# Eight list tiles beside the first sort, the sort's prefix sums re-placed, and a third product added on VectorE

## The chip, the cores and the metric

The kernel runs on one core of a Trainium2 chip. The metric is the device time of one execution in microseconds (us). TensorE is called PE, VectorE DVE, ScalarE ACT, GpSimd POOL and SyncE SP. Times inside a run are counted from the start of the profiled span.

## The reference

One graph-attention layer over 4096 nodes with 512 features and 8 heads. The adjacency matrix `adj` (4096 x 4096, int32) is sparse: each row has some 10 to 40 non-zero entries, and only these take part in the row's softmax.

```python
hs = layer_norm(x, ln1);  ht = layer_norm(h_target, ln1)      # both masked by nodemask
q = (ht @ Wq + bq) / 8;  k = hs @ Wk + bk;  v = hs @ Wv + bv  # 8 heads of 64
probs = softmax(where(adj != 0, q @ k.T, -1e30))              # per head
ht = ht + (probs @ v) @ Wo + bo
ht = layer_norm(ht, ln2)
y = ht + gelu(ht @ W1) @ W2
out = layernorm(x + y)
```

## The kernel before

All matrix products are in fp32. Rows are taken in tiles of 128.

**Lists.** `edges(i)` reads the adjacency of row tile i in four quarters of 128 x 1024 int32 (512 KB each, issued on SP by `quarter`, L714). ACT turns a quarter into signs (L733, into one of three `signs` places) and adds up the degree. DVE multiplies the signs by column numbers (L740), takes the eight largest of each segment (three L742 a quarter), and at the end of the tile decodes them and picks the 24 largest (the tail, L749 to L766) into a record. `rest_d` receives the leftovers (L773, on SP). Quarters lie in eight places of a ring; those of the last tile that is read ahead of attention lie in two `wide` places. The first 16 tiles are part A, the other 16 part B (`NA` is 16).

**Sort.** `sort(part)` orders a part's rows by degree: a one-hot matrix `oh` (L834), its column totals by a matmul with ones (L845), a prefix scan on DVE (L846), a second matmul with a triangular matrix `lower` (L853), additions and a reduce, and a cast to the rank (L857). POOL then scatters the 16 records of 128 rows into DRAM (L861). After sorting, each tile of 128 rows has a known largest degree (its cap, 11 to 39), and tiles are taken in the order that `_order` gives: tiles 0 to 15 are of part A, 16 to 31 of part B. Two tiles make a feed-forward group.

**Projections.** `project` makes k and v of all 4096 rows: 16 steps of 2 tiles, with x loaded on SP (L882), normalised (DVE statistics, L697 to L692, POOL power L687, ACT L898), transposed and multiplied (L912, L937), copied by ACT (L939) and stored into `kvd` in DRAM.

**Attention.** For each tile, `front` fetches the rows of h_target that the records name, ties itself to the last projection (L1003, `latest`), normalises (ACT L1007), transposes (L1011, L1014) and multiplies with Wq (L1020, L1025). Then the edges are taken in groups of up to S = 3: POOL gathers one k and v row per node and edge from `kvd` (L975, 512 KB per gather, into 17 ring places for part A and 20 for part B), DVE multiplies with q (L1228) and reduces to logits (L1233), ACT takes the exponential (L1237, L1246), DVE multiplies the first two v rows by the probabilities (L1192), ACT the third (`by_scalar`, L1209 and L1212). In part B the first two products are added on DVE (L1196). PE adds the products up in PSUM by transposing matmuls (L1200), four of 128 x 128 per product that is left. `finish` and `feed` do the rest: Wo, norm, and the feed-forward with W1 and W2 (L1333, GELU on ACT L1336, L1342).

**Order.** `_weave` decides the order in which the parts are written: each part is a generator that yields a cost, and the one with the least cost so far goes on. First `projections`, `prepare` (part A's lists, sort, first fronts) and `fill` (the first `FILL` tiles of part B's lists) are woven; then attention, the feed-forward, `other_lists` (the other lists of part B, from cost `WAIT` = 100 on, then their sort) and late weights. A planner then orders each engine's queue; `behind(ins)` adds the constraint that an instruction comes after another one on its engine. Each queue runs in its order.

Of the kernel before, what the change touches and what calls it, by code (L numbers as in the profile page):

```python
# [8 lines left out]
F32 = mybir.dt.float32  # L9
# [3 lines left out]
ALU = mybir.AluOpType  # L13
# [4 lines left out]
P = 128  # L18
# [359 lines left out]
DEG, TGT, ROW, RST, E0 = 0, 1, 2, 3, 5  # L378
# [65 lines left out]
def adj_resnorm_kernel(  # L444
# [33 lines left out]
    nc = tc.nc  # L478
    N, D = x.shape
# [3 lines left out]
    NT = N // P  # L483
# [7 lines left out]
    SQ = 3  # L491
# [6 lines left out]
    for g in groups:  # L498
        i0 = GROUPS[-1][-1] + 1 if GROUPS else 0
        GROUPS.append(list(range(i0, i0 + len(g))))  # L500
    NA, NBT = len(CAPS_A), len(CAPS_B)
    PARTS = ((0, len(CAPS_A)), (len(CAPS_A), len(CAPS_B)))
    S = 3
# [29 lines left out]
    with tc.tile_pool(name="keep", bufs=1) as keep:  # L533
# [17 lines left out]
        with ExitStack() as late:  # L551
# [121 lines left out]
            def rstd_of(pool, mv, n, name):  # L673

                rs = power(pool, mv, n, name)
                return rs, negmean(pool, mv, rs, n, name)
# [6 lines left out]
            def power(pool, mv, n, name, ve=None):  # L683
                if ve is None:
                    ve = shifted(pool, mv, n, name)
                rs = pool.tile([P, n], F32, name=name + "_rs")
                nc.gpsimd.tensor_tensor(rs, ve, mhalf[:, :n], ALU.pow)  # L687
                return rs

            def negmean(pool, mv, rs, n, name):  # L690
                nm = pool.tile([P, n], F32, name=name + "_nm")
                nc.vector.scalar_tensor_tensor(nm, mv[:, :, 0], -1.0, rs, op0=ALU.mult, op1=ALU.mult)  # L692
                return nm
# [4 lines left out]
                nc.vector.bn_aggr(mv, st)  # L698


            held, moms = [], list(range(NT))
            mvh = wp.tile([P, NT, 2], F32, name="mvh")

            adjs = []
            DEEP = 8
            FILL = 6
            RINGED = NA + FILL - 1

            def quarter(i, h):
# [7 lines left out]
            def behind(ins):  # L717
                return tc.issue_after(ins[-1]) if ins else nullcontext()

            def edges(i):  # L720

                part = 1 if i >= NA else 0
                rec = Rs[part][:, i - PARTS[part][0], :]
                cand = lp.tile([P, SEG, 8], U16, name="cand", bufs=2)
                for h in range(NQ):
                    n = i * NQ + h
                    while len(adjs) < min(n + 2, NT * NQ):
                        adjs.append(quarter(*divmod(len(adjs), NQ)))
                    a, adjs[n] = adjs[n], None

                    sg = turn_of("signs", signs)
                    with behind(newest if i >= NA else []):
                        nc.scalar.activation(sg, a, AF.Sign, accum_out=dpart[:, i, h:h + 1])  # L733
                    ahead = min(n + DEEP - 1, n + 3 + n // 2)
                    while len(adjs) < min(max(n + 3, min(ahead, RINGED * NQ)), NT * NQ):
                        adjs.append(quarter(*divmod(len(adjs), NQ)))
                    yield 0.0 if i < NA else 1.0
                    wd = sg.bitcast(U16)
                    with behind(logits):
                        nc.vector.tensor_tensor(wd, wd, lio, ALU.mult)  # L740
                    for s, (w0, w1) in enumerate(SEGS):
                        nc.vector.max(cand[:, h * SQ + s, :], wd[:, w0:w1])  # L742
                    if h == 1:
                        keep_rest()
                    if h % 2 and moms:
                        moments(moms.pop(0))
                    yield 2.0 if i < NA else 1.0
                dec = dec_w
                nc.vector.tensor_single_scalar(dec[:, 0], cand, 255, op=ALU.bitwise_and)  # L749
                nc.vector.tensor_single_scalar(dec[:, 1], cand, 8, op=ALU.logical_shift_right)  # L750
                gid = lp.tile([P, 2 * SEG, 8], F32, name="gid")
                dec = dec.rearrange("p b s e -> p (b s) e")
                off = segoff.rearrange("p b q s -> p (b q s)")
                nc.vector.scalar_tensor_tensor(gid, dec, 0.0,
                                               off.unsqueeze(2).to_broadcast([P, 2 * SEG, 8]),
                                               op0=ALU.is_gt, op1=ALU.mult)
                nc.vector.scalar_tensor_tensor(gid, dec, 2.0, gid, op0=ALU.mult, op1=ALU.add)
                flat = gid.rearrange("p s e -> p (s e)")
                for r in range(RE // 8):
                    top = rec[:, E0 + r * 8:E0 + (r + 1) * 8]  # L760
                    nc.vector.max(top, flat)
                    if r + 1 < RE // 8:
                        nc.vector.match_replace(flat, top, flat, 0.0)
                held.append((rest_d[i * P:(i + 1) * P, :], flat))
                has = lp.tile([P, MAXE], F32, name="ehas")
                nc.vector.tensor_scalar(has[:, :RE], rec[:, E0:E0 + RE], 0.0, 0.0, op0=ALU.is_gt,  # L766
                                        op1=ALU.add, accum_out=cnt[:, i:i + 1])
                yield 4.0

            def keep_rest():  # L770

# [42 lines left out]
            def sort(part):  # L814
# [23 lines left out]
                pos = pos[:, :NB * n].rearrange("p (b i) -> p b i", b=NB)  # L838
                posf = pos.rearrange("p b i -> p (b i)")
                w = NB * n // 2  # L840
                yield 6.0
                for c in range(2):
                    sl = slice(c * w, (c + 1) * w)
                    pt = ps.tile([P, w], F32, name="t", bufs=2)
                    nc.tensor.matmul(pt, ones_bf, ohf[:, sl], start=True, stop=True)  # L845
                    nc.vector.tensor_tensor_scan(posf[:, sl], one_c.to_broadcast([P, w]), pt,  # L846
                                                 0.0 if c == 0 else posf[:, c * w - 1:c * w],
                                                 op0=ALU.mult, op1=ALU.add)
                yield 4.0
                for c in range(2):  # L850
                    sl = slice(c * w, (c + 1) * w)
# [323 lines left out]
            def attention():  # L1175
# [10 lines left out]
                def values(i, j0, n, kv, p, cps, after):  # L1186

                    m = n - 1 if n == S else n  # L1190
                    v4 = kv[:, :m, D:].rearrange("p j (h d) -> p j h d", h=H)
                    nc.vector.tensor_tensor(v4, v4, p[:, j0:j0 + m, :].unsqueeze(3)  # L1192
                                            .to_broadcast([P, m, H, HD]), ALU.mult)
                    slots = list(range(n))
                    if m > 1 and i >= NA:
                        nc.vector.tensor_add(kv[:, 0, D:], kv[:, 0, D:], kv[:, 1, D:])  # L1196
                        slots.remove(1)
                    for j in slots:
                        for c in range(KC):
                            nc.tensor.matmul(cps[:, c, :], kv[:, j, D + c * P:D + (c + 1) * P], ident,  # L1200
                                             is_transpose=True, start=j0 + j == 0 and c == 0,
                                             stop=j0 + n == TILES[i][1] and j == slots[-1],
                                             skip_group_check=True)
                    if after is not None:
                        tails.append(after)
# [181 lines left out]

            WAIT = 100.0
            AHEAD = 4
            UNIT = 60.0  # L1390

            ed = all_edges()
# [16 lines left out]
            def prepare():  # L1409

                yield from _take(ed, NA * steps)
                ready.append("lists")
                while moms:
                    moments(moms.pop(0))
                rs, nm = rstd_of(wp, mvh, NT, "n0")
                for R, (i0, n) in zip(Rs, PARTS):
                    Rf = R.bitcast(F32)
                    nc.vector.tensor_copy(Rf[:, :, RST], rs[:, i0:i0 + n])
                    nc.vector.tensor_copy(Rf[:, :, RST + 1], nm[:, i0:i0 + n])
                nm = turn_of("wide", wide)  # L1420
                nc.sync.dma_start(nm[:NT, :P], nodemask.rearrange("(c p) -> c p", p=P))
                nmf = nm.bitcast(F32)[:NT, P:2 * P]
                nc.vector.tensor_scalar(nmf, nm[:NT, :P], 1.0, None, op0=ALU.not_equal)
                nc.vector.tensor_reduce(bad[:NT, 0:1], nmf, AX.X, ALU.max)
                yield from sort(0)
                yield from first_fronts()

            def fill():

                while not ready:  # L1430
                    yield None
                yield 9.0
                for cost in _take(ed, FILL * steps):
                    yield cost

# [15 lines left out]

            def other_lists():
                for cost in ed:
                    yield 1.8 * cost
                keep_rest()
                yield from sort(1)

# [37 lines left out]
```

## Time and profile before

| | |
|---|---|
| three runs, median | 1816.04 us (1813.79 to 1820.43) |
| profiled execution | 1813.07 us, its span 1811.3 us |
| busy us: PE / DVE / ACT / POOL | 1678.3 / 1397.6 / 1224.7 / 967.4 |
| DMA | 461.03 MB, mean 255 GB/s |
| L1200, transposes into PSUM | x2008 |
| L1196, additions of two products | x101, 680 ns |
| last projection matmul ends | 267.5 us |
| first gather issued, first L1228 | 271.5 us, 295.3 us |

A busy share is an average over stages: projections and part A's lists up to about 267 us, then attention with the feed-forward beside it up to about 1670, then the feed-forward alone. Matmuls are pipelined, so a mean duration on PE is a latency and not the distance between two matmuls. Idle time on an engine that is not the bound costs nothing.

### The profile page before, as it was taken

To read this page: it belongs to the slowest core of one execution; us is meant where nothing else is said; L and a number is where in the kernel's file an instruction comes from. 1 tells how busy PE (TensorE), PEld (TensorE's weight loads), DVE (VectorE), ACT (ScalarE), POOL (GpSimd) and SP (SyncE) were. 2 spreads that over 40 slices of the span, in tenths; PEclk is the share of its full clock that TensorE was granted. 3 is DMA by queue.
4 is the path that set the end of the run, shared out by engine and by line. 5 is a ranking of instruction groups with operands and counts; after the bars stand their busy time and mean duration, and the time that the engine had idled before them with its cause. 6 is when DMAs were issued, how large, how long until landed. Compare 5 with 4: busy or idle time off the path is not lost. (4 is left out here: it accounts for less than half of the span.)

```text
span 1811.3 us, 22772 instructions
## 1 busy us (share of the span) xinstructions
PE 1678.3 (93%) x7030; PEld 1096.2 (61%) x7030; DVE 1397.6 (77%) x2404; ACT 1224.7 (68%) x3121; POOL 967.4 (53%) x818
## 2 busy tenths in 40 slices
PE   7999994697998999998999989989999999999995
PEld 3444442565665666675676756656666666666663
DVE  6887568989987879886969989897969797988100
ACT  5776464677786887675868767777858676776210
POOL 1000155756455556787677788867566665762101
PEclk9999995898999999999999999999999999999998
DMA  9999879888778697678788888777677776772000
GB/s 344 365 377 359 306 260 357 304 274 311 268 247 304 239 336 237 219 239 278 276 284 286 276 274 277 251 271 271 205 254 227 266 262 232 256 245 92 24 1 26
DMA packets 142060, 461.03 MB, mean 255 GB/s; under 512 B 18548, under 2 KB 23496, under 8 KB 141928
## 3 DMA queue, kind: packets, MB, share of 16 engines
q0 software_dynamic: 96144, 342.27, 55.6%
q1 hardware_dynamic: 37968, 94.12, 14.7%
q10 hardware_dynamic: 7816, 23.08, 3.3%
q8 instruction: 58, 0.95, 0.2%
q14 instruction: 74, 0.61, 0.1%
HBM read 430.61 MB, written 28.79 MB: 254 GB/s over the span
## 5 line engine op out<-in xcount | busy, mean ns | idle before, releaser
L975 POOL DMA_INDIRECT kv<-kvd,rec x603 | 753.4, 1249 | 355.8 <-PE cps L1200 166.5
L1333 PE MATMUL pf<-h2T,w 128*128 128x256 f32 (+1 forms) x2176 | 466.4, 368 | 0.6 <-ACT h2T L1155 0.6
L1342 PE MATMUL po<-w,gt 128*128 128x512 f32 x1024 | 461.4, 593 | 5.6 <-ACT gt L1336 5.6
L1333 PEld LDWEIGHTS pf<-h2T,w 128*128 128x128 f32 x2176 | 389.6, 191 | 64.9 <-issue 20.1
L1228 DVE TENSOR_TENSOR kv<-kv,tq 128x1536 f32<-128x1536 f32 (+2 forms) x211 | 351.6, 1676 | 61.9 <-DMA kv<-kvd,rec 49.2
L1212 ACT ACTIVATE kv<-kv,pa 128x64 f32<-128x64 f32 x1520 | 391.8, 337 | 4.6
L1233 DVE TENSOR_REDUCE lg<-kv 128x24 f32<-128x1536 f32 (+2 forms) x211 | 350.1, 1666 | 1.3
L1200 PE MATMUL cps<-ident,kv 128*128 128x128 f32 x2008 | 264.9, 280 | 47.0 <-DVE kv L1192 39.5
L1200 PEld LDWEIGHTS cps<-ident,kv 128*128 128x128 f32 x2008 | 239.1, 144 | 113.2 <-issue 44.6
L1342 PEld LDWEIGHTS po<-w,gt 128*128 128x128 f32 x1024 | 187.0, 190 | 198.9 <-issue 191.3
L1192 DVE TENSOR_TENSOR kv<-kv,p 128x1024 f32<-128x1024 f32 (+1 forms) x211 | 250.9, 1193 | 25.3 <-ACT p L1237 25.2
L687 POOL TENSOR_TENSOR n_rs<-n_ve,mhalf 128x2 f32<-128x2 f32 (+2 forms) x51 | 45.8, 897 | 337.2 <-DVE n_ve L680 172.8
L733 ACT ACTIVATE kv<-kv 128x1024 uint8<-128x1024 int32 x128 | 134.5, 1053 | 67.1 <-DMA kv<-in_adj_dram 34.6
L1020 PE MATMUL t<-wq,tq 128*128 128x512 f32 x256 | 126.1, 640 | 19.8 <-ACT tq L1014 19.8
L1336 ACT ACTIVATE gt<-pf 128x512 f32<-128x512 f32 x128 | 76.4, 597 | 93.8 <-PE pf L1333 90.3
L1336 ACT ACT_TABLE_LOAD x104 | 133.4, 1283 | 1.7
L937 PE MATMUL pq<-wk,h2T 128*128 128x512 f32 x256 | 118.7, 607 | 8.2 <-ACT tq L939 4.5
L937 PE MATMUL pq<-wv,h2T 128*128 128x512 f32 x256 | 115.4, 593 | 1.5 <-ACT tq L939 0.7
L1124 PE MATMUL t<-wo,rb 128*128 128x512 f32 x256 | 115.2, 593 | 0.0
L742 DVE MAX8 cand<-kv 128x8 uint16<-128x171 uint16 (+1 forms) x384 | 109.1, 324 | 1.2
L1237 ACT ACTIVATE p<-lg 128x24 f32<-128x24 f32 (+2 forms) x179 | 39.0, 218 | 100.1 <-DVE lg L1233 99.3
L1020 PEld LDWEIGHTS t<-wq,tq 128*128 128x128 f32 x256 | 51.3, 206 | 79.9 <-issue 47.0
(160 smaller groups left out, 1541.0 us busy)
## 6 DMA issues: line engine op xcount, KB each, us to landing
kv<-in_adj_dram SPq DMA_DIRECT2D x128, 512.0 KB, 7.1
kvd<-tq ACTq DMA_DIRECT2D x24, 512.0 KB, 6.9
kv<-kvd,rec POOLq DMA_INDIRECT x603, 5.9
kv<-in_L_gnn_h_target_dram SPq DMA_DIRECT2D x32, 256.0 KB, 7.2
kv<-in_x_dram SPq DMA_DIRECT2D x15, 512.0 KB, 8.7
w<-in_L_gnn_W_dram SPq DMA_DIRECT2D x4, 1024.0 KB, 12.4
kvd<-kv ACTq DMA_DIRECT2D x8, 512.0 KB, 3.2
w<-in_L_gnn_W_dram ACTq DMA_DIRECT2D x4, 1024.0 KB, 7.3
```

The lines of the kernel that those rows point to most:

```text
L733: nc.scalar.activation(sg, a, AF.Sign, accum_out=dpart[:, i, h:h + 1])
L937: nc.tensor.matmul(pkv, hT[:, kc, j * P:(j + 1) * P], w[:, kc, :], start=kc == 0, stop=kc == KC - 1)
L975: issues[:] = [nc.gpsimd.indirect_dma_start(out=dst, out_offset=None, in_=table[:, :], in_offset=bass.IndirectOffsetOnAxis(ap=idx, axis=0) ...
L1020: nc.tensor.matmul(pq, hT[:, kc, :], wq[:, kc, :], start=kc == 0, stop=kc == KC - 1)
L1192: nc.vector.tensor_tensor(v4, v4, p[:, j0:j0 + m, :].unsqueeze(3) .to_broadcast([P, m, H, HD]), ALU.mult)
L1200: nc.tensor.matmul(cps[:, c, :], kv[:, j, D + c * P:D + (c + 1) * P], ident, is_transpose=True, start=j0 + j == 0 and c == 0, stop=j0 + n ...
L1212: newest[:] = [nc.scalar.mul(v, v, pa[:, hd:hd + 1]).ins]
L1228: nc.vector.tensor_tensor(kv[:, :n, :D], kv[:, :n, :D], tq[:, :D].unsqueeze(1).to_broadcast([P, n, D]), ALU.mult)
L1233: logits[:] = [nc.vector.tensor_reduce(lg[:, :n, :], kv[:, :n, :D].rearrange("p j (h d) -> p j h d", h=H), AX.X, ALU.add).ins]
L1333: nc.tensor.matmul(pf[:, k, :], w1[(f0 + k) // KC][:, kc, (f0 + k) % KC * P:((f0 + k) % KC + 1) * P], h2T[:, kc, :w], start=kc == 0, stop= ...
L1336: nc.scalar.activation(gt, pf, AF.Gelu_apprx_tanh)
L1342: nc.tensor.matmul(po[j], gt[:, k, j * P:(j + 1) * P], w2[(f0 + k) // KC][:, (f0 + k) % KC, :], start=False, stop=f0 + k == FC - 1, skip_g ...
```

## The change

- `FILL` goes from 6 to 8: eight tiles of part B have their lists made ahead of attention. Their costs in the weave go down (quarters 0.7 and 0.7 instead of 1.0 and 1.0, the tail 2.4 instead of 4.0), `fill` starts at 1.0 instead of 9.0, and part A's quarters count 1.8 instead of 2.0. `other_lists` counts 2.2 instead of 1.8 times the cost.
- In the first sort both totals (L845) are written right after 2.0 instead of 6.0, into the PSUM places `cps`, and the scans come after another 6.0, behind the latest max (L742) of the lists.
- The layer-norm factors of h_target (L692 on 32 columns, L1418, L1419) are taken out of `prepare` and written behind the first sort's scans.
- From tile 21 on (`DENSE`), in every second full group of three, a further L1196 adds the third product to the sum on DVE, and PE transposes one product instead of two.

```diff
-            FILL = 6
+            FILL = 8
...
-                    yield 0.0 if i < NA else 1.0
+                    yield 0.0 if i < NA else 0.7 if i < NA + FILL else 1.0
...
-                        nc.vector.max(cand[:, h * SQ + s, :], wd[:, w0:w1])
+                        maxima[:] = [nc.vector.max(cand[:, h * SQ + s, :], wd[:, w0:w1]).ins]
...
-                    yield 2.0 if i < NA else 1.0
+                    yield 1.8 if i < NA else 0.7 if i < NA + FILL else 1.0
...
-                yield 4.0
+                yield 2.4 if NA <= i < NA + FILL else 4.0
...
-                yield 6.0
+                yield 6.0 if part else 2.0
+                tots = []
                 for c in range(2):
                     sl = slice(c * w, (c + 1) * w)
-                    pt = ps.tile([P, w], F32, name="t", bufs=2)
+                    pt = ps.tile([P, w], F32, name="t" if part else "cps", bufs=2)
                     nc.tensor.matmul(pt, ones_bf, ohf[:, sl], start=True, stop=True)
-                    nc.vector.tensor_tensor_scan(posf[:, sl], one_c.to_broadcast([P, w]), pt,
-                                                 0.0 if c == 0 else posf[:, c * w - 1:c * w],
-                                                 op0=ALU.mult, op1=ALU.add)
+                    tots.append((sl, pt))
+                if not part:
+                    yield 6.0
+                for c, (sl, pt) in enumerate(tots):
+                    with behind([] if part else maxima):
+                        scan = nc.vector.tensor_tensor_scan(
+                            posf[:, sl], one_c.to_broadcast([P, w]), pt,
+                            0.0 if c == 0 else posf[:, c * w - 1:c * w],
+                            op0=ALU.mult, op1=ALU.add)
+                while factors:
+                    with behind([scan.ins]):
+                        factors.pop()()
...
+                        if n == S and i >= DENSE and j0 // S % 2:
+                            nc.vector.tensor_add(kv[:, 0, D:], kv[:, 0, D:], kv[:, S - 1, D:])
+                            slots.remove(S - 1)
...
+            DENSE = 21
...
-                rs, nm = rstd_of(wp, mvh, NT, "n0")
-                for R, (i0, n) in zip(Rs, PARTS):
-                    Rf = R.bitcast(F32)
-                    nc.vector.tensor_copy(Rf[:, :, RST], rs[:, i0:i0 + n])
-                    nc.vector.tensor_copy(Rf[:, :, RST + 1], nm[:, i0:i0 + n])
+                rs = power(wp, mvh, NT, "n0")
+
+                def rest_of_factors():
+                    nm = negmean(wp, mvh, rs, NT, "n0")
+                    for R, (i0, n) in zip(Rs, PARTS):
+                        Rf = R.bitcast(F32)
+                        nc.vector.tensor_copy(Rf[:, :, RST], rs[:, i0:i0 + n])
+                        nc.vector.tensor_copy(Rf[:, :, RST + 1], nm[:, i0:i0 + n])
+
+                factors.append(rest_of_factors)
...
-                yield 9.0
+                yield 1.0
...
-                    yield 1.8 * cost
+                    yield 2.2 * cost
```

More of the change, by code (lines that the diff above doesn't have):

```diff
@@ L698, in stats @@
                 nc.vector.bn_aggr(mv, st)
-            held, moms = [], list(range(NT))
+            held, moms, factors, maxima = [], list(range(NT)), [], []
             mvh = wp.tile([P, NT, 2], F32, name="mvh")
```

## The prediction

> **What bounds the kernel now.** I read the page's 40 slices first, then the stages (busy time by window), then the timeline of each engine around the hole.
>
> ```profile
> PE   7999994697998999998999989989999999999995
> ...
> PEclk9999995898999999999999999999999999999998
> ```
>
> Each digit is a tenth of a 45.3 us slice. TensorE is nearly full except in slices 7 and 8, where its clock drops too. The stages say how much is lost, and how full the others are (columns: stage; its length, then PE, weight load, DVE, ACT and POOL busy us with instruction counts; clock; DMA share; GB/s):
>
> ```profile
> 200.00:250.00 50.00, 49.49 (x142) 23.54 (x141) 23.04 (x74) 24.58 (x47) 16.15 (x18) 1.00 0.70 250
> ...
> 270.00:290.00 20.00, 10.52 (x22) 4.30 (x20) 13.62 (x54) 12.75 (x28) 15.08 (x16) 0.72 0.92 334
> 290.00:310.00 20.00, 2.82 (x12) 2.42 (x12) 18.02 (x37) 7.14 (x25) 4.63 (x5) 0.50 0.99 376
> 310.00:330.00 20.00, 9.92 (x40) 7.91 (x41) 19.12 (x23) 8.37 (x32) 14.11 (x11) 0.59 0.97 368
> ...
> 1450.00:1550.00 100.00, 100.00 (x436) 68.56 (x435) 81.27 (x96) 73.51 (x201) 60.98 (x54) 1.00 0.74 247
> ```
>
> Between 270 and 330 PE stands idle for 60 - 23.3 = 36.7 us while DVE and DMA are full; between 200 and 250 DVE is half empty and DMA has 30% free. From 1350 to 1640 PE is full (289.8 of 290 us) and DVE is not. After attention (about 1670) PE runs only the feed-forward to the end. So PE is the bound, and its idle time before that moves the end. (The page's own chain covers the last 3 us only.) The hole in lines of the timelines (start, length, engine, line; in brackets the idle before and who ended it):
>
> ```profile
> 224.11 0.95 DVE L846 TENSOR_TENSOR_SCAN kv<-one_c,t 128x384 f32<-128x384 f32 x1 [13.01 <-PE t L845]
> 229.82 0.17 DVE L857 CAST kv<-kv 128x16 int32<-128x16 f32 x1
> 271.53 0.94 POOL L975 DMA_INDIRECT kv<-kvd,rec  x1 [0.56 <-issue]
> 289.83 1.06 ACT L733 ACTIVATE kv<-kv 128x1024 uint8<-128x1024 int32 x1 [5.50 <-DMA kv<-in_adj_dram]
> 295.34 1.74 DVE L1228 TENSOR_TENSOR kv<-kv,tq 128x1536 f32<-128x1536 f32 x1
> 305.25 2.82 PE L1200 MATMUL cps<-ident,kv 128*128 128x128 f32 x12 [21.88 <-DVE kv L1192]
> ```
>
> DVE waits 13.01 us for the sort's first matmul, which stands behind projections on PE. Projections end at 267.5 and the first gather leaves at 271.5, yet attention's first product (L1228) runs at 295.34: six lists of part B (235 to 294, 9.8 us each) lie ahead of it on DVE, and the last one's quarter reached ACT late. The sort itself is not the last wait: its records fetch h_target rows by 262.7, before the projections end.
>
> **What the Trainium skill says.** "TensorE: Matmul & The Clock Gate", What's actually happening: an idle window of about 3.4 us halves PE's clock; the trace agrees (0.50 in 290:310). The same page, Architectural detail: ACT and DVE are strict FIFO; here ACT's 5.50 us wait held all behind it. "VectorE: DVE Perf Modes", TRN2 errata: an fp32 tensor_tensor of 512 takes (512+151)/0.96 = 691 ns; L1196 has a median of 680. "DMA: Bandwidth & Descriptors", Issuing engines are not separate DMA queues: SP, ACT and POOL share 16 engines; here 400 to 419 GB/s from 285 to 305 with all three loading.
>
> **The change, part by part.** Line numbers are those of before; the walks use the changed program's engine order.
>
> (a) Eight lists instead of six ahead of attention, beginning where DVE idled. A list is 4 loads of 512 KB, 4 Signs (1053 + 191 ns), 4 scale-and-max rounds (1.17 us) and a tail (L749 to L766, 3.4 us; 252.09 to 255.47): 8.1 us of DVE alone. Mixed with another list's rounds it is less: 277.57 to 281.95 held a tail and two rounds, 4.4 us instead of 5.8. The new order mixes about half, so 7.2 us each.
> Signs of list 16 now follow the copies ready at 209.2, one batch behind each projection tile: about 211 instead of 233.8. DVE: four rounds to 217; sort arithmetic (two scans, two adds, product, reduce, cast, factors) 6.2 us within list 17; the cast at about 227 (before 229.82). Then seven lists, less the last one's two rounds and tail. That reaches `front`'s tie L1003 at 217 + 6.2 + 6.5 x 7.2 = 270, against 268.17.
> On ACT the last list's third and fourth Signs stand ahead of L1007. Their loads take places that its first two Signs free at 265; landing takes 7.2 us (as at 282.59 to 289.83), so both end at 274.7, and L1007 starts there, not at 268.62: 6 us late. From there, as before: transposes, L1014 2.87 us, L1020 for one tile 4.9 us; L1025 at 284.7 and L1228 at **285.4 instead of 295.3: 10 us earlier**. List 21's rest inside attention (296.99 to 312: 3.3 us and a wait of 0.91) is gone too: 14.
> But gathers set a second limit. They issue from about 273.5, one per 1.25 us; a gather is 0.5 MB, 1.25 us at 400 GB/s, and the 4 MB of late weights (ACT queue, after the first scalar products) take 10 us of it. The 17th lands at about 310. The seventh group, at 318.62 before, then runs at 308 to 312. I take **-9**, bounds -14 and -2.
>
> (b) Two lists less inside attention: 2 x 8 us of DVE and 2 x 5 us of ACT leave the stretch 375 to 850. There PE was idle 17 us (400:600) and 10.5 us (600:900), mostly for gathers and logits. Pace 2.2 on 8 lists (8 x 26.4 = 211 cost units) ends with 1.8 on 10 (216), so the second sort and its POOL scatters stay where they were. **-4**; bounds 0 and -8.
>
> (c) Three products added. Full groups of 3 with odd index in tiles 21 to 31: 28. Each drops 4 PE transposes and adds one DVE add.
>
> ```profile
> L1200 PE MATMUL cps<-ident,kv 128*128 128x128 f32 x2008 | 264.9, 280 | 47.0 <-DVE kv L1192 39.5 <-DVE kv L1196 7.3
> L1196 DVE TENSOR_TENSOR kv<-kv 128x512 f32<-128x512 f32 x101 | 68.4, 680 | 0.3
> ```
>
> 280 ns is a pipelined latency; eight transposes at 1454.11 hand over at 1454.98, so 0.109 us each: 112 x 0.109 = 12.2 us of PE. DVE pays 28 x 0.61 (its start-to-start) = 17 us. These tiles run from about 1177 to 1670. From 1350 on PE is full and DVE has 14 to 19% free, so two thirds count in full; from 1177 to 1350 DVE is 75 to 95% busy and the gain is doubtful. POOL already waits 34.4 us on L1196 (26 times) to reuse ring places; the added instruction lengthens that by 0.6 us per group, behind four groups of prefetch. **-10**; bounds -13 and +5 (all on DVE, less the PE time).
>
> (d) The sort. Its two totals move from 223.75 to about 209.2 on PE; `oh` was ready at 210.6. DVE no longer waits for the 5.43 us power ahead of it (L692 moves behind the scans), and the store that L754 waited for (to 205.78) stands ahead of the weight load on SP now, so `oh` comes at 204 to 210.6: PE stalls 0 to 1.5 us. New wait: the scans stand behind list 16's last max, and both L853 products need the PSUM places the scans free. PE reaches them at 217.7, the scans end at 218 and 219. Behind L853 on PE are the projections, and all of attention behind those. **+1**; bounds 0 and +6. The factors only have to be written before the scatters (L861). The last x load moves 4 adjacency loads back on SP, 2 MB or 5.5 us; its transposes (216) have 11 us of slack: 0, covered by PE's queued projections; without that cover up to 3 us inside (d)'s bound.
>
> Sum: -9 - 4 - 10 + 1 = **-22 us**. The profiled execution took 1813.07 us (span 1811.3 and 1.8 around it), so it becomes 1791. It lies 3.0 below the median of the runs, 1816.04; on the median's scale I predict **1794**.
>
> **Rivals.**
> Larger gain: gathers don't hold the ramp (-14), the lighter DVE fills PE's gaps (-8), all transposes count (-12), +1: -33, **1783**. For it: DVE waited only 0.88 us for gathers up to 330. Against: DMA already ran at 0.92 to 0.99 there.
> No change: the ramp is bound by transfers (-2), DVE takes back what lists free (-1), and the added products fall in groups where DVE comes last (-2): -5, **1811**. For it: DVE 92% busy in 1000:1200. Against: PE full from 1350.
> Slower: the lists pile up ahead of attention. DVE works them off in order ahead of the tie, and the three `signs` places hold ACT, with the projections' copies behind it, at DVE's pace. At today's 9.8 us a list the tie is at 217 + 6.2 + 6.5 x 9.8 = 287, and L1228, 15 us after the tie as in (a), at 302: 7 late. At 13 us it is at 323, 28 late; with -13 from the other parts that is +15, **1831**. It decides above some 12.1 us a list (L1228 22 late). For it: today's 9.8, and 4 MB more traffic before 270. Against: much of the 9.8 is waiting for ACT, whose Signs come earlier.
> That the change does nothing is excluded: the order shows eight lists and 112 fewer transposes.
>
> **How the numbers follow.** 0.5% is 9 us, about what a measurement of this kernel can tell from no change. Main case (1786 to 1805) 0.61, larger gain 0.14, no change 0.17, slower 0.08. So faster 0.75, same 0.17, slower 0.08. The range, 1777 to 1812, leaves out the slower case, the top of no change and the far end of the larger gain.
>
> **What would show it.** Right: L846 ends its 13.01 us wait at about 217; L857 near 227; first L1228 near 285; less than 30 us of PE idle in 270:330; 1896 transposes in L1200's group and PE still full from 1350. Wrong: the tie after 275, an ACT wait above 8 us on adjacency ahead of L1007, PE waiting at L853 by more than 3 us, or DVE above 95% with PE gaps after 1350.

## The result, and the profile after

The changed kernel takes 1803.15 us (median of 6 runs, 1799.61 to 1806.98), the kernel before beside it 1816.58 us (6 runs): ratio **0.9924**, interval 0.9905 to 0.9943, 13 us less. In a second comparison, beside three relatives, it took 1815.39 us against 1819.57 us: ratio **0.9979**, interval 0.9961 to 0.9997, 4 us less. The two intervals do not meet. So an interval covers the scatter of one comparison and not the difference between comparisons (whether the chip makes it is not shown). The kernel is faster by 4 to 13 us, and below, kernels are compared first with those measured beside them on the same chip. The profiled execution of after took 1805.56 us (span 1803.8).

Of the page of after, the same two rows of 40 slices (a slice is now 45.1 us). The hole in slices 7 and 8 is still there.

```profile
PE   7989984697999999998999999989999999999995
...
PEclk9999997898999999999999999989999999999998
```

The same stages by window (length, then busy us and counts of PE, weight load, DVE, ACT and POOL; clock; DMA share; GB/s):

```profile
200.00:250.00 50.00, 47.49 (x138) 22.46 (x137) 33.97 (x127) 30.16 (x58) 17.30 (x18) 1.00 0.93 330
270.00:290.00 20.00, 11.65 (x27) 5.31 (x26) 14.42 (x59) 11.95 (x24) 7.74 (x8) 0.74 0.76 254
290.00:310.00 20.00, 9.55 (x41) 6.41 (x40) 17.21 (x13) 7.34 (x31) 16.00 (x14) 0.89 1.03 406
310.00:330.00 20.00, 6.83 (x34) 6.03 (x32) 14.90 (x16) 7.71 (x30) 13.36 (x11) 0.51 1.03 401
1450.00:1550.00 100.00, 100.00 (x418) 67.05 (x417) 88.67 (x109) 74.88 (x202) 64.41 (x53) 1.00 0.75 250
```

DVE is no longer half empty in 200:250 (33.97 us instead of 23.04): the lists moved there. But PE now loses 2.5 us in that window and is idle for 32.0 us in 270:330 (36.7 before). From 290 to 330 the DMA engines are full at 401 to 406 GB/s and DVE is not. From 290 to 450 DVE waits 12.4 us for gathers, where before waited 6.7: more of the ramp waits for transfers.

Lines of after's timelines that answer to those of the hole before (start, length, engine, line; in brackets the idle before and who ended it):

```profile
216.41 0.93 DVE L852 TENSOR_TENSOR_SCAN kv<-one_c,cps 128x384 f32<-128x384 f32 x1
226.12 0.16 DVE L867 CAST kv<-kv 128x16 int32<-128x16 f32 x1
271.81 3.70 PE L947 MATMUL pq<-wv,h2T 128*128 128x512 f32 x8 [0.60 <-ACT kv L949]
282.58 0.94 POOL L985 DMA_INDIRECT kv<-kvd,rec  x1 [1.11 <-DMA kv<-in_adj_dram]
292.07 1.76 DVE L1241 TENSOR_TENSOR kv<-kv,tq 128x1536 f32<-128x1536 f32 x1 [0.71 <-DMA kv<-kvd,rec]
299.07 2.82 PE L1213 MATMUL cps<-ident,kv 128*128 128x128 f32 x12 [5.08 <-DVE kv L1202]
```

The 13.01 us that DVE waited for the totals are gone and the cast (L857, now L867) comes 3.7 us earlier. Yet the last projection ends at 271.81 + 3.70 = 275.5 instead of 267.5, the first gather leaves at 282.58 instead of 271.53, and the first product (L1228, now L1241) runs at 292.07 instead of 295.34, just after the gather that it needs.

The groups of the transposes and of the additions (L1200 and L1196, now L1213, L1206 and the new L1209; count, busy us, mean ns, idle before and its releasers):

```profile
L1213 PE MATMUL cps<-ident,kv 128*128 128x128 f32 x1896 | 252.5, 280 | 34.4 <-DVE kv L1202 23.6 <-DVE kv L1206 7.8 <-issue 2.5
L1206 DVE TENSOR_TENSOR kv<-kv 128x512 f32<-128x512 f32 x101 | 68.7, 684 | 0.3
L1209 DVE TENSOR_TENSOR kv<-kv 128x512 f32<-128x512 f32 x28 | 19.2, 685 | 0.1
```

112 transposes fewer and 28 additions more, as written.

### The profile page after: what moved, and what is told of

Same layout as the page of the kernel before. It is cut to its first block, busy times and chain, and to the rows that moved or that the text cites. A ratio compares the mean times of both kernels' runs of the same rounds, so it can differ in the third digit from the quotient of the medians.

```text
span 1803.8 us, 22591 instructions
## 1 busy us (share of the span) xinstructions
PE 1666.8 (92%) x6918; PEld 1081.8 (60%) x6918; DVE 1413.1 (78%) x2432; ACT 1224.5 (68%) x3121; POOL 971.4 (54%) x818
## 5 line engine op out<-in xcount | busy, mean ns | idle before, releaser
L1241 DVE TENSOR_TENSOR kv<-kv,tq 128x1536 f32<-128x1536 f32 (+2 forms) x211 | 352.0, 1677 | 78.7 <-DMA kv<-kvd,rec 63.1
L1213 PEld LDWEIGHTS cps<-ident,kv 128*128 128x128 f32 x1896 | 226.9, 145 | 99.5 <-issue 45.7
L1213 PE MATMUL cps<-ident,kv 128*128 128x128 f32 x1896 | 252.5, 280 | 34.4 <-DVE kv L1202 23.6
L687 POOL TENSOR_TENSOR n_rs<-n_ve,mhalf 128x2 f32<-128x2 f32 (+2 forms) x51 | 48.9, 958 | 345.1 <-DVE n_ve L680 153.6
L733 ACT ACTIVATE kv<-kv 128x1024 uint8<-128x1024 int32 x128 | 134.5, 1053 | 59.6 <-DMA kv<-in_adj_dram 22.3
L1134 PE MATMUL t<-wo,rb 128*128 128x512 f32 x256 | 115.5, 592 | 0.0
L742 DVE MAX8 cand<-kv 128x8 uint16<-128x171 uint16 (+1 forms) x384 | 108.2, 325 | 6.2 <-remote 2.4
```

What stands on the lines that cost most here:

```text
L1241: nc.vector.tensor_tensor(kv[:, :n, :D], kv[:, :n, :D], tq[:, :D].unsqueeze(1).to_broadcast([P, n, D]), ALU.mult)
```

## The experiments

Three groups of four kernels; each group ran on one chip, beside runs of the kernel before (medians 1818.87, 1819.57 and 1817.31 us). Gains in us below are (1 - ratio) times that median.

### First group: the parts one by one

**c_only**, the kernel before with part (c):

```diff
                         slots.remove(1)
+                        if n == S and i >= DENSE and j0 // S % 2:
+                            nc.vector.tensor_add(kv[:, 0, D:], kv[:, 0, D:], kv[:, S - 1, D:])
+                            slots.remove(S - 1)
```

> The kernel before with the third product's addition alone (DENSE = 21), lists and sort as before. Theory 1 (the whole gain is the 112 transposes, since between the two traces PE's busy time fell by 11.5 us and its idle time grew by 4): 10 to 13 us less than before, ratio 0.9930 to 0.9945, and the milestones of tiles 0 to 20 unmoved. Theory 2 (the products pay only because two lists fewer inside attention left DVE room): 0 to 5 us less, ratio 0.997 to 1.000, with new waits of PE for DVE after 1177 us.

Measured: 1813.1 us, ratio 0.9970 (0.9953 to 0.9988), 5.5 us less. Between the two theories; the added products pay without fewer lists, but about half of what they were forecast.

**no_c**, the changed kernel without them:

```diff
-                        if n == S and i >= DENSE and j0 // S % 2:
-                            nc.vector.tensor_add(kv[:, 0, D:], kv[:, 0, D:], kv[:, S - 1, D:])
-                            slots.remove(S - 1)
```

> The changed kernel without the third product's addition: eight lists and the re-placed sort remain. Theory 1: no gain or a small loss, 0 to 5 us more than before, ratio 1.000 to 1.003, last projection matmul still late, near 275 us. Theory 2 (lists and sort pay what the forecast said, -9 - 4 + 1): 12 us less, ratio 0.9935.

Measured: 1807.21 us, ratio 0.9938 (0.9913 to 0.9963), 11 us less. Theory 1 falls. It came from comparing PE's busy time in two single profiles, and that total is no steady quantity: after and after_again below have the same instructions and show 1666.8 and 1675.6 us.

**sort_only**, no_c with six lists and their old costs, so that the sort's change is left:

```diff
-            FILL = 8
+            FILL = 6
...
-                    yield 0.0 if i < NA else 0.7 if i < NA + FILL else 1.0
+                    yield 0.0 if i < NA else 1.0
...
-                    yield 1.8 if i < NA else 0.7 if i < NA + FILL else 1.0
+                    yield 2.0 if i < NA else 1.0
...
-                yield 2.4 if NA <= i < NA + FILL else 4.0
+                yield 4.0
...
-                yield 1.0
+                yield 9.0
...
-                    yield 2.2 * cost
+                    yield 1.8 * cost
```

> The kernel before with the sort's change alone (totals written after 2.0, factors behind the scans), six lists with their old costs. Theory 1: within 3 us of before, cast of the rank a few us earlier, projections ending at 267 to 269 us as before. Rival: the sort is what pays and the lists lose it again; then 5 us or more less than before, with the first gather earlier than 271.5 us.

Measured: 1818.63 us, ratio 0.9984 (0.9968 to 1.0001), within 3 us. The cast came at 233.7, not earlier than before.

**lists_only**, the opposite: the kernel before with these six lines as the change has them, and the old sort (two of the six are shown, the others are those of sort_only the other way round):

```diff
-            FILL = 6
+            FILL = 8
...
-                    yield 2.0 if i < NA else 1.0
+                    yield 1.8 if i < NA else 0.7 if i < NA + FILL else 1.0
```

> The kernel before with FILL = 8 and the new costs of the lists, and the sort as before. Theory 1 (Signs placed ahead of the projections' copies in ACT's queue hold the projections): last projection matmul 5 us or more later than 267.5, total 0 to 6 us more than before. Theory 2: 10 us less than before. Rival 3 (without the moved sort the added lists stand ahead of the scans on DVE and delay the records): slower than before by 8 us or more.

Measured: 1810.24 us, ratio 0.9933 (0.9904 to 0.9961), 12 us less; last projection at 270.3, first product at 286.6. Theory 1 falls, theory 2 is nearest, rival 3 falls. The gain of no_c is in the lists' edits.

### Second group: more additions, and one number of the lists' edits alone

**after_again** is the changed kernel.

> The changed kernel once more, beside its two relatives below on the same chip. 1803 us is 13 less than before; lists and sort alone measured 0.9938, so the third product's addition has 0 to 6 us of that. Theory 1 (the added products pay about half of the forecast's 10): ratio 0.991 to 0.992. Theory 2 (with the lists in place they pay next to nothing): 0.993 to 0.994.

Measured: 0.9979 (0.9961 to 0.9997), outside both. It is the yardstick for this group.

**dense_all**, the changed kernel with

```diff
-                        if n == S and i >= DENSE and j0 // S % 2:
+                        if n == S and i >= DENSE:
```

> The changed kernel with the addition in all full groups of tiles 21 to 31: 63 instead of 28, so another 140 transposes (140 x 0.109 = 15 us of PE) go and DVE gets 35 x 0.61 = 21 us more. Theory 1 (PE is the bound there, and a dropped transpose counts at 40 to 100%): 6 to 15 us less than the changed kernel, ratio to before 0.984 to 0.989. Theory 2 (PE's freed time turns into waiting, because DVE and the gathers behind its ring places can't run faster): 0 to 10 us more than the changed kernel, ratio 0.992 to 0.998, with PE no longer full after 1350 and DVE above 95%.

Measured: 1808.53 us, ratio 0.9937 (0.9907 to 0.9967): 7.6 us less than after_again (the intervals overlap by a little), on theory 1's side.

**dense_b**, the same with

```diff
-            DENSE = 21
+            DENSE = 16
```

> The same in all 95 full groups of part B (tiles 16 to 31): 268 transposes fewer than in the changed kernel (29 us of PE), DVE + 41 us. Theory 1: 10 to 25 us less than the changed kernel, ratio to before 0.979 to 0.987. Theory 2: in 1000 to 1200, where DVE is already 92 to 97% busy, every further addition delays the stage: 5 to 25 us more than the changed kernel, ratio 0.995 to 1.006.

Measured: 1823.27 us, ratio 1.0020 (1.0003 to 1.0038): 15 us more than dense_all. Theory 2 has the total. Its own windows show what the 380 transposes fewer than before turned into:

```profile
1000.00:1177.00 177.00, 161.37 (x644) 105.23 (x644) 165.61 (x187) 132.73 (x358) 134.61 (x91) 0.96 0.74 247
1177.00:1350.00 173.00, 159.37 (x614) 102.15 (x613) 158.38 (x187) 131.61 (x345) 130.72 (x92) 0.95 0.75 247
1350.00:1640.00 290.00, 265.44 (x1020) 170.88 (x1019) 261.95 (x315) 219.91 (x572) 219.71 (x158) 0.95 0.77 253
```

PE is idle for 54 of these 640 us (17 in before), and its clock, 1.00 after 1350 in before, is 0.95. DVE is 90 to 94% busy, not full. The waits of the same stretch, 1000 to 1640, of dense_b (engine, line, whom it waited for; us, times, longest), from the views of PE, DVE and ACT:

```profile
PE cps L1213 <- DVE kv L1209: 24.0, 9, 7.7
PE t L1161 <- ACT h L1152: 20.6, 3, 7.7
```

```profile
DVE n_nm L692 <- POOL n_rs L687: 41.6, 6, 9.2
```

```profile
ACT h L1152 <- DVE n_nm L692: 41.3, 6, 9.2
```

Before has waits of these kinds too, but there DVE waits 22.3 us for the power (L687), PE waits 7.3 us for an addition, and PE never waits for h. One spot of dense_b on DVE and PE, then what stands ahead of the power on POOL:

```profile
1451.84 0.16 DVE L692 SCALAR_TENSOR_TENSOR n_nm<-mv,n_rs 128x2 f32<-128x2 f32 x1 [9.16 <-POOL n_rs L687]
1454.45 1.12 PE L1213 MATMUL cps<-ident,kv 128*128 128x128 f32 x4 [7.70 <-DVE kv L1209]
```

```profile
1450.12 0.94 POOL L985 DMA_INDIRECT kv<-kvd,rec  x1 [0.30 <-issue]
1451.09 0.72 POOL L687 TENSOR_TENSOR n_rs<-n_ve,mhalf 128x2 f32<-128x2 f32 x1
```

The power of a norm stands in POOL's queue behind gathers that leave one per 1.25 us. DVE's L692 waits 9.16 us for it, the next product and the added addition (L1209) stand behind L692 on DVE, and PE waits 7.70 us for the addition. The wait of 6.11 us at 1281.64 is of the same kind. These two, 13.8 of PE's 24.0 us, and the 20.6 us for h (each wait follows one of DVE for the power) are one chain: POOL's queue, the power, DVE's queue, then ACT or PE. Here the order of the queues limits, and not DVE's share. POOL also waits for ring places that additions hold, 31.5 us, but before had 34.4 us of that, and none of the gathers directly ahead of the power waits longer than 0.31 us for such a place.

The 32 groups that dense_b adds to dense_all all lie in tiles 16 to 20, so the dose and the place changed together. The loss shows behind them: from the 20th to the 32nd tile's product with Wo (L1134) dense_b takes 500.7 us and dense_all 480.8, with the same additions in all but one of these tiles. What carries the loss over is not shown.

**parta18**, the kernel before with one number changed:

```diff
-                    yield 2.0 if i < NA else 1.0
+                    yield 1.8 if i < NA else 1.0
```

> The kernel before with part A's quarters at 1.8 instead of 2.0 in the weave and nothing else. In the profiles PE was full in 50:100 in the three kernels with 1.8 (50.0 us) and not in the three with 2.0 (48.5 to 48.7). Theory 1 (part of what the lists gain is made there, ahead of any list of part B): 3 to 6 us less than before, ratio 0.9965 to 0.9985, and projections that end 2 to 4 us earlier. Theory 2 (the stage is bound by transfers, and its order is indifferent): within 2 us of before, ratio 0.999 to 1.001.

Measured: 1809.54 us, ratio **0.9944** (0.9929 to 0.9960), 10 us less, and 6 us less than the whole change on this chip (after_again; the intervals are barely apart). More than theory 1 expected; but its second half failed, the projections end at 268.4. What moved is the sort. First before, then parta18, on PE (the totals L845) and DVE (the first scan, the addition after L853, the cast, the first product):

```profile
223.75 0.49 PE L845 MATMUL t<-oh,ones_bf 128*128 128x384 bf16 x2
```

```profile
207.28 0.49 PE L845 MATMUL t<-oh,ones_bf 128*128 128x384 bf16 x2
```

```profile
207.64 0.95 DVE L846 TENSOR_TENSOR_SCAN kv<-one_c,t 128x384 f32<-128x384 f32 x1 [0.84 <-PE t L845]
...
215.71 1.02 DVE L854 TENSOR_TENSOR kv<-cps,kv 128x384 f32<-128x384 f32 x2 [6.00 <-PE cps L853]
...
219.26 0.17 DVE L857 CAST kv<-kv 128x16 int32<-128x16 f32 x1
...
281.37 1.74 DVE L1228 TENSOR_TENSOR kv<-kv,tq 128x1536 f32<-128x1536 f32 x1
```

With 1.8, part A's lists count less in the weave, so they end sooner (`oh`, the matrix that the totals need, begins at 201.8 instead of 209.7), and the sort stands on PE one step of projections sooner. The scans wait 0.84 us instead of 13.01. The cast gains 10.6 us and not all of the 16.5, because DVE now waits 6.00 us for L853, which PE reaches at 215.3. List 16's first Sign runs at 217.0 instead of 233.8, and the first product at 281.4 instead of 295.3, with six lists and the old sort.

### Third group: what the eight lists add, and the best combination

**after_20**, the changed kernel with that number back at 2.0:

```diff
-                    yield 1.8 if i < NA else 0.7 if i < NA + FILL else 1.0
+                    yield 2.0 if i < NA else 0.7 if i < NA + FILL else 1.0
```

> The changed kernel with part A's quarters back at 2.0 in the weave; eight lists, the sort's change and the added products stay. Theory 1 (the gain at the start of attention comes from the 1.8, which puts the sort a projection tile earlier, not from the eight lists): the rank's cast at 230 us or later, and 4 to 10 us more than the changed kernel, ratio to before 0.999 to 1.004. Theory 2 (the eight lists, which begin where DVE idled, make it): within 2 us of the changed kernel, ratio 0.993 to 0.998.

Measured: 1814.09 us, ratio 0.9980 (0.9964 to 0.9997). The total stands on theory 2's edge, just short of theory 1's, and does not decide: it equals after_again, and is 10 us above the first comparison of after. The start is theory 1's: cast at 240.2, first product at 310.4.

**after_fill6**, the changed kernel with six lists:

```diff
-            FILL = 8
+            FILL = 6
...
-                    yield 2.2 * cost
+                    yield 1.8 * cost
```

> The changed kernel with six lists ahead of attention instead of eight, and 1.8 instead of 2.2 as the pace of the others, so that the second sort stays where it was. Theory 1 (eight lists take back in the projections what they save later: three or four Signs stand ahead of each pair of copies in ACT's queue): projections end at 268 to 271 us instead of 275, and the total is the changed kernel's or up to 6 us less, ratio 0.991 to 0.998. Theory 2 (the forecast's: two lists are worth 4 us inside attention and several ahead of it): 4 to 9 us more than the changed kernel, ratio 0.999 to 1.002.

Measured: 1805.26 us, ratio 0.9939 (0.9914 to 0.9963), 11 us less than before. The forecast's theory falls: taking two lists back costs nothing that can be seen. Theory 1 has the total, but not the reason: the projections end at 275.6 with six lists too.

**p18_c**, parta18 with part (c), and **p18_dense**, parta18 with the additions in all 63 groups, that is, with one line different:

```diff
-                        if n == S and i >= DENSE and j0 // S % 2:
+                        if n == S and i >= DENSE:
```

> The kernel before with two parts of the change alone: part A's quarters at 1.8, and the third product's addition in the same 28 groups. The 1.8 alone measured 0.9944, the addition alone 0.9970. Theory 1 (the two are independent): 0.9905 to 0.9925. Theory 2 (the addition's freed PE time turns into waiting once the start is earlier): 0.9935 to 0.9955.

> The same with the addition in all 63 full groups of tiles 21 to 31, the version that the runs so far point to: 0.9944 from the 1.8, and with eight lists the 63 groups measured 0.9937 beside 0.9979 for 28. Theory 1: less than both kernels, ratio 0.987 to 0.991. Theory 2 (PE's idle time after 1350, 11 us with 63 groups, eats what they save): 0.992 to 0.996.

Measured: 1804.79 us, ratio 0.9931 (0.9907 to 0.9954), and 1800.25 us, ratio **0.9914** (0.9888 to 0.9939). Both lie between their two theories: on top of the 1.8 the additions seem to bring less than alone (p18_c is 0.0013 below parta18, c_only 0.0030 below before; the first two ran on different chips). p18_dense is the fastest kernel of the study, 16 us less than before, with six lists and the old sort. It is ahead of the changed kernel's second comparison, and not to be told from the first, nor from the 1.8 alone (parta18).

### The start of attention in all profiles

One execution each. Before and c_only have the same code up to attention, and so have no_c, after, after_again, dense_all and dense_b: their spread is the scatter.

| part A, lists, sort | cast of the rank | last projection ends | first product |
|---|---|---|---|
| 2.0, six, old (before, c_only) | 229.8, 231.1 | 267.5, 270.4 | 295.3, 305.0 |
| 2.0, six, new (sort_only) | 233.7 | 269.8 | 302.7 |
| 2.0, eight, new (after_20) | 240.2 | 280.3 | 310.4 |
| 1.8, six, old (parta18, p18_c, p18_dense) | 216.9 to 220.9 | 267.6 to 271.8 | 280.7 to 285.1 |
| 1.8, eight, old (lists_only) | 221.4 | 270.3 | 286.6 |
| 1.8, six, new (after_fill6) | 226.3 | 275.6 | 287.8 |
| 1.8, eight, new (no_c, after, after_again, dense_all, dense_b) | 222.8 to 227.3 | 272.1 to 276.8 | 288.8 to 293.3 |

Every kernel with 1.8 starts attention earlier than every one with 2.0. Among those with 1.8, eight lists and the new sort each go with a start some microseconds later, in so few executions.

How much of the head start lasts can be read from the products with Wo, which PE makes once per tile, in order. The first and the fourth of before, then of parta18:

```profile
340.88 3.60 PE L1124 MATMUL t<-wo,rb 128*128 128x512 f32 x8
447.73 3.60 PE L1124 MATMUL t<-wo,rb 128*128 128x512 f32 x8
```

```profile
329.34 1.02 PE L1124 MATMUL t<-wo,rb 128*128 128x512 f32 x2
442.86 3.60 PE L1124 MATMUL t<-wo,rb 128*128 128x512 f32 x8
```

The lead of 11.5 us is 4.9 us three tiles later. In the mean, before, c_only and sort_only begin the first product with Wo at 346.3 and the fourth at 452.4. The four kernels with 1.8 and the old sort begin them at 330.6 and 445.4: of 16 us, 7 are left. The six with 1.8 and the new sort begin them at 337.2 and 451.8: of 9 us, less than 1 is left, so in these six single executions the start does not account for what no_c and after gained over many. The DMA engines are full from 290 to 330 in parta18 (403 and 405 GB/s, share 1.03) as in after, where before has 376 and 368, which fits a ramp that transfers then hold.

## Why the prediction was right, and where it was not

The direction held, and in the first comparison the range; 1815.39 us of the second lies above it. The size was 13 (or 4) us for a forecast of 22. That the total came inside the range is in part luck: the terms do not stand up one by one.

**(a), the start.** Right: the first Sign of list 16 (forecast 211, measured 210.52), the scans (217, 216.41), the cast (227, 226.12), and that gathers would limit next (L1241's last wait is for a gather). Wrong: the tie at 270 came at 278.49, and all after it 7 us late (L1035 forecast 284.7, measured 290.66; L1241 285.4, 292.07), and PE's idle time in 270:330 is 32.0 us where less than 30 was forecast. The step that failed is "217 + 6.2 + 6.5 x 7.2". The 6.5 lists took 55.3 us, 8.5 each. DVE stood idle for 7.4 us of them, and without that a list takes 7.4: its work was sized rightly, its waits were put at nothing. 6.4 of the 7.4 us lie between 240 and 250, and the tie follows the lists without a gap. Of after's DVE timeline:

```profile
243.88 0.81 DVE L742 MAX8 cand<-kv 128x8 uint16<-128x171 uint16 x3 [1.68 <-issue]
...
247.41 0.81 DVE L742 MAX8 cand<-kv 128x8 uint16<-128x171 uint16 x3 [2.39 <-remote]
...
277.76 0.81 DVE L742 MAX8 cand<-kv 128x8 uint16<-128x171 uint16 x3
278.49 0.20 DVE L1013 SCALAR_TENSOR_TENSOR rec<-rec,kv 128x2 f32<-128x2 f32 x1
```

ACT and PE stood at the same time. Lines of its ACT timeline, and one of its PE timeline:

```profile
248.81 0.59 ACT L949 COPY kv<-pq 128x512 f32<-128x512 f32 x1 [5.80 <-issue]
...
253.64 1.06 ACT L733 ACTIVATE kv<-kv 128x1024 uint8<-128x1024 int32 x1 [0.56 <-ACT kv L733]
...
254.69 1.05 ACT L949 COPY kv<-pq 128x512 f32<-128x512 f32 x2
```

```profile
255.31 3.70 PE L947 MATMUL pq<-wv,h2T 128*128 128x512 f32 x8 [2.17 <-ACT kv L949]
```

What held the three engines around 245 the trace does not name ("issue" is time in which an engine waited for nothing that the profile shows, and "remote" names no instruction). DVE waits of this kind ahead of L742, 3.4 to 7.0 us in sum, stand in all the profiles with 1.8 and either eight lists or the new sort, and once in c_only (4.6), whose code here is that of before; the other six have none. The walk also kept the projections' end at 267.5, and it came at 275.5: PE is idle for 6.9 us in 240:275, where before had none until 267.5. 4.4 us of these are waits for copies that stand behind Signs in ACT's queue (254.69 above is one), 2.5 us have no named releaser. The projections end late where the new sort stands beside lists at 0.7 (272.1 to 276.8, and 275.6 with six lists), not with either alone (269.8 in sort_only, 270.3 in lists_only); why is open, and the new sort with 1.8 and lists at 1.0 was not run.

The larger error of (a) is the cause. The first product comes 14 us sooner, at 281.4 instead of 295.3, from the 1.8 alone, a number that the prediction took for part of eight lists. The walk contained it, since it used the changed order, but no step priced it. Measured alone it is worth 10 us; lists and sort with it 11 to 12 (no_c, lists_only). So -9 for the start was near the measured gain for another reason than the one given. What eight lists and the new sort add beyond the 1.8 is not told from nothing in the first and third groups, and in the second the whole change was 6 us behind the 1.8 alone. Two readings in the prediction were loose: DVE was not full in 270:330 (50.8 of 60 us), and DMA moved 393 GB/s from 300 to 305.

**(b), two lists fewer inside attention.** Forecast -4; measured nothing that stands out of the scatter. PE's idle time in 450:1177 is 26.2 to 29.8 us in the seven kernels with six lists (mean 28.6), 24.7 to 31.2 in the six with eight (27.5; dense_b, which adds products there, is left out). From the fourth to the 16th product with Wo the kernels with six lists take 584.4 us in the mean, those with eight 584.1. DVE lost 16 us of work in 450:1000 (457 us in before, 441 in after), but PE's idle time hardly shows it.

**(c), the products.** Forecast -10; measured 5.5 alone, less on top of the 1.8 (ratio 0.9931 after 0.9944), as far as two chips can be compared. The step that failed is "two thirds count in full": PE's idle time in 1177:1640 was 6.4 to 11.8 us in the five kernels without the addition (mean 8.4), 10.4 to 16.8 in the six with 28 (13.4), 20 in both with 63, and 38 with 95. So of 12.2 us about 5 come back as waiting, of 27.5 about 12, and of 41.4 about 30, with another 8 in 1000:1177. The stage itself says the same: from the 20th to the 32nd product with Wo it takes 492.0 us in the mean without the addition, 485.6 with 28 groups, 480.8 and 480.9 with 63, and 500.7 with 95. For 28 groups, what is saved (6.4) and what comes back as waiting (5.0) make 11.4 us, so the estimate of 12.2 us for the transposes stands. DVE's free share after 1350 was no measure of it. With 63 groups 7.7 and 7.3 us of PE's waits are for the added addition itself; with 28 none is, and what takes the 5 us back there is spread over waits that the other kernels have too. And PE slows down with its gaps: "TensorE: Matmul & The Clock Gate", What's actually happening, in the Trainium skill, has an idle window of about 3.4 us halve the clock; the trace agrees, with waits up to 7.7 us and a granted clock of 0.95 after 1350 in dense_b.

**(d), the sort.** Forecast +1; alone it measured -3, its interval reaching to 0. PE did not wait at L853 (now L863) in after; the longest such wait in a relative is 2.96 us (after_fill6). But the move replaces a wait that the 1.8 removes by itself, and with the 1.8 the old sort's cast comes 1 to 10 us sooner than the new one's.

**The rivals.** "Slower, lists piling up" needed 12.1 us a list; they took 8.5: no pile. Of the signs of a wrong forecast one was there, the tie after 275. "No change" (-5) is what the second comparison shows; its first reason, the ramp bound by transfers, is seen in both profiles of after (DMA share 1.03 from 290 to 330).

## What to carry to other kernels

A change of several edits has to be priced edit by edit, the small numbers of a scheduler too: here one weight, 2.0 to 1.8, moved a sort past one step of projections, and no kernel that has it together with the rest is clearly faster than it alone. A head start is not yet a gain: look again some tiles later, here three, what is left of it. When an engine is full, an instruction taken from it counts only as far as the chains that feed it have slack; read this from who waits for whom and try twice and three times the dose, since the gain turned between 63 and 95 groups. A forecast walk has to carry every queue that its new work is put into, and its waits: here DVE's lists, which did their work in 7.4 us each but took 8.5, and ACT's queue, where projection copies stood behind the added Signs.

## What the runs showed of the hardware that was not expected

- One kernel against the same other kernel gave 0.9924 and 0.9979 in two comparisons, with intervals of +-0.2%. In the second, single executions ranged over 1805 to 1828 us. The mean granted clock differs too: 0.971 over the first six executions of after, 0.966 over the 22 of the second. Which is cause and which effect is open.
- PE's busy time for the same instructions differs between executions: 1666.8 us at a mean clock of 0.974, 1675.6 at 0.968. It is no measure of work to better than 9 us.
- Gaps go with a lower clock: dense_b, with 54 us of PE idle in 1000:1640, has a mean clock of 0.960 over its 14 executions, dense_all, with 23 us, 0.966 over nine. In the two profiles the 128 transposes that dense_b has less, 14.0 us at 0.109, took only 5.1 us from PE's busy time; but that difference lies inside the 9 us above.
